# Moving the second sequence's transposes of a first feed-forward from TensorE to 32x32 squares and 16 DMAs

## The chip, the cores and the metric

The kernel runs on one core of one Trainium2 chip. The metric is the time of one execution on the device in microseconds (us). Three runs of the kernel before are at hand, and one more execution was taken with the hardware profiler; all readings of durations come from that one. Engines are called PE (TensorE; PEld is its weight load), ACT (ScalarE), DVE (VectorE), POOL (GpSimd) and SP (SyncE, which here only issues DMAs).

## The reference

Two transformer layers with a layer norm behind each of four steps, on 2 sequences of 512 rows with 512 columns. What bears on the change is the end of the first attention and the first feed-forward:

```python
x = _layernorm(x + _L0_attn_ref(x, ...))     # linear attention that reads a memory M with 8 heads
x = _layernorm(x + _L0_ffn_ref(x, w_gate, w_up, w_down))
x = _layernorm(x + _L1_attn_ref(x, ...))     # softmax attention, one head of 128
x = _layernorm(x + _L1_ffn_ref(x, ...))      # SwiGLU feed-forward, 1376 wide

def _L0_ffn_ref(x, w_gate, w_up, w_down):    # the weights are ternary: -s, 0 or s
    xf = x.astype(jnp.float32) / 128.0
    gate = jnp.einsum('bsh,ih->bsi', xf, w_gate)
    up = jnp.einsum('bsh,ih->bsi', xf, w_up)
    inter = jax.nn.silu(gate) * up
    inter_q = jnp.trunc(jnp.clip(inter * 128.0, -128.0, 127.0)).astype(jnp.int8)
    down = jnp.einsum('bsi,hi->bsh', inter_q.astype(jnp.float32), w_down)
    return jnp.trunc(jnp.clip(down * 128.0, -128.0, 127.0)).astype(jnp.int8)
```

## The kernel before

The rows of the two sequences lie in eight tiles of 128 rows by 512 columns, four for each sequence (`order` lists them, sequence 0 first). Matrix products contract over the partitions, so each step needs the rows transposed: 512 columns become four blocks of 128 partitions (`NK`), each with 512 rows side by side.

**Reading the attention's memory** (`read`, L392 to L428) goes tile by tile. PE makes eight products of a tile, one for each head, into eight PSUM banks. ACT takes the denominators from them (L405), DVE inverts these (L409), and the products are scaled and added to the row tile: three by ACT (L414) and summed by POOL (L418), five by DVE in place (L423). At the end POOL adds the sum of the three to the tile (L427). One tile later `norm_a0` (L495) normalizes the tile: statistics on DVE (L135, L137), root on POOL (L143, L144), an offset on DVE (L503), and the norm itself on ACT (L504). For the last tile it follows at once. In between, ACT and DVE also check and divide the ternary weights: `check_up` compares, and `divided` (L506) writes a chunk of gate and up weights divided by its scale, two activations for each of 11 chunks of 128 inner columns. Three chunks are asked for within this loop, the others in the feed-forward; the order on ACT and DVE is a planner's, which moves what is ready forward, so that some are done earlier.

**Splitting the rows** (`split`, L254) serves the first feed-forward. For each of the four blocks, PE makes four transposes into a PSUM bank (L264), ACT copies the bank rounded to the fast float format (`xh`, L265), and DVE writes what the rounding left (`xl`, L266). The first sequence's blocks are made inside the reading, the second's inside the feed-forward.

**The first feed-forward.** `up(b, c)` (L560) makes, for sequence b and chunk c, eight gate products (`pg_f`, L567: xh and xl of four blocks) and eight up products (`pu_f`), in one of two ways that a flag chooses. ACT then applies Silu (L583), DVE multiplies (L586) and cuts to 12 bits (L155), ACT makes two truncated halves (L165, L166) and DVE joins them (L593). The order of these calls is written out by hand at the end (L675 to L725): three chunks of the first sequence, the second sequence's split, a fourth chunk of the first, then three chunks of the second, and from there in turns. Each `up` also divides one further half chunk of weights (`to_divide`).

Beside it goes the preparation of the down weights. SP loads eleven chunks (`down_weights`, L248). DVE takes the largest value of the first chunk (`largest`, `mx_d`), PE and DVE make one scale of it (`over_partitions`, `scales`, which gives `inv_d`), POOL divides the eleven chunks by it (`check_down`, L435), DVE compares each (L204), and `verdict` makes the flag for `down`. The divided down weights lie in the places of up weights that are no longer needed. `f0_down` then makes the down products, the residual sum and the norm of each tile.

Pools matter for the change. `xtp` has two places of 8 KB a partition (tag "xt"), used by transposed rows. `wop` has six places of 4 KB (`pair_tile`), `wqp` four of the same size (`query_tile`). PSUM has eight banks, of which an `up` holds two.

A `with tc.issue_after(step.ins)` puts the instructions inside it behind `step` on its own engine's queue, without a wait. POOL's queue is in the order of the program.

Of the kernel before, what the change touches and what calls it, by code (L numbers as in the profile page):

```python
# [19 lines left out]
P = 128  # L20
# [9 lines left out]
LAST = HID - 1  # L30
LENT = 3
# [5 lines left out]
def kernel(  # L37
# [118 lines left out]

    def truncated_parts(pool, y, n, name):

        a = pool.tile([P, S], I8, tag="tr_a", name=f"ta_{name}")
        b = pool.tile([P, S], I16, tag="tr_b", name=f"tb_{name}")
        nc.scalar.activation(a[:n], y, AF.Relu, bias=below_half[:n])  # L165
        nc.scalar.activation(b[:n], y, AF.Relu, bias=below_half[:n], scale=-1.0)  # L166
        return a, b
# [86 lines left out]
    def split(b):  # L254

        hi = xtp.tile([P, NK, S], F32, tag="xt", name=f"xh_{b}").bitcast(F32R)
        los = [pair_tile(f"xl_{b}_{i}").bitcast(F32R) for i in range(2)]
        his = [hi[:, k, :] for k in range(NK)]
        los = [los[k // 2][:, k % 2, :] for k in range(NK)]

        def block(k):
            pt = psum(f"pt_f0{b}_{k}")
            for t in range(NT):
                nc.tensor.transpose(pt[:, ts(t, P)], xs[b][t][:, ts(k, P)], ident)  # L264
            nc.scalar.copy(his[k], pt)  # L265
            nc.vector.tensor_sub(los[k], pt, his[k].bitcast(F32))  # L266

        return his + los, block

# [11 lines left out]
    with tc.tile_pool(name="a0w", bufs=1) as a0w, tc.tile_pool(name="a0", bufs=2) as a0:  # L281
# [110 lines left out]
        def read(b, t, between):  # L392
# [34 lines left out]
            nc.gpsimd.tensor_add(x[:, :LAST], x[:, :LAST], ys[0][:, :LAST])  # L427
# [38 lines left out]
        for h in range(NH):  # L466
            queries(1, xt1, h)
            if h == 0:
                sum_weights(nc.vector, 4)
                sum_weights(nc.gpsimd, 5)  # L470
                fold(0)
                fold(1)
                mx_up = largest(
                    [gus[0][:, a].rearrange("p k i -> p (k i)") for a in range(2)], "up"
                )
# [71 lines left out]

    wdp = ctx.enter_context(tc.tile_pool(name="wdp", bufs=1))
    wds = down_weights(wd0_in, "0")
    with tc.tile_pool(name="f0", bufs=2) as f0:  # L550
# [9 lines left out]
        def up(b, c, behind=()):  # L560
# [19 lines left out]
            with ExitStack() as tied:  # L580
# [3 lines left out]
            y = f0.tile([P, S], F32, tag="y", name=f"y_f0{b}_{c}")  # L584

            step = nc.vector.scalar_tensor_tensor(  # L586
                y[:n], sg[:n], eff_up[:n, 1:2], pp[1][:n], ALU.mult, ALU.mult
            )
# [46 lines left out]
        pds, ys, stats, moved = {}, {}, {}, {}  # L635

        def scaled(i):
            y = f0.tile([P, HID], F32, tag="y", name=f"yd_{i}")
            moved[i] = nc.scalar.activation(y, pds[i], AF.Copy, scale=down_scale)
# [47 lines left out]
        top_d = over_partitions(mx_d, "down")  # L687
        for c in range(4, 8):
            up(0, c)
            if c == 4:  # L690
                sc_d, inv_d = scales(top_d, "down")
            up(1, c - 1)
            for i in range(2 * c - 8, 2 * c - 6):
                check_down(i)
        up(0, 8)
        up(1, 7)
        check_down(8)
        check_down(9)
        up(0, 9)
        check_down(10)  # L700
        up(0, 10)
        tot_d = total(counts_d, "down")
        up(1, 8)
# [3 lines left out]
        up(1, 9)  # L707
# [4 lines left out]
        up(1, 10, moved.values())  # L712
# [568 lines left out]
```

## Time and profile before

| what | value |
|---|---|
| median of 3 runs | 472.01 us (471.8, 472.01 and 799.53) |
| the profiled execution | 471.99 us, of which the span from first to last instruction is 470.0 us |
| PE busy / DVE busy / ACT busy / POOL busy | 463.0 / 327.9 / 268.1 / 114.4 us |
| granted TensorE clock | 0.996 |
| reading of the memory, first to last product | about 72 to 131 us |
| up part of the first feed-forward | about 131 to 219 us |
| down weights, SP's loads | 137.7 to 143.5 us |

The span is what the profile sees; some 2 us lie around it. A busy share is a mean over stages with different limits, so the stage around the change is read by itself, by its windows and by the chain of waits. A PE that is busy is not always at its own pace, since the ends of matrix products are modelled.

### The profile page before, as it was taken

What the parts mean: (1) busy time and instruction counts of PE and PEld (TensorE: products, weight loads), DVE (VectorE), ACT (ScalarE), POOL (GpSimd) and SP (SyncE); (2) the same over time, 40 slices, a digit from 0 to 9 for tenths busy, and PEclk for the clock granted to TensorE, in tenths of its full rate; (3) what the DMA queues carried; (4) which work ended last, traced back from release to release, by engine and by line L of the source; (5) the groups of instructions that cost most, each with busy time, mean ns of one, the idle gap of its engine ahead of it and who ended that gap; (6) DMA issues with size and microseconds to landing.
All of it is one profiled execution on the core that took longest, in us unless ns stands there. A gap on an engine that the chain in (4) does not pass through costs nothing.

```text
span 470.0 us, 5725 instructions
## 1 busy us (share of the span) xinstructions
PE 463.0 (99%) x1899; PEld 330.7 (70%) x1899; DVE 327.9 (70%) x622; ACT 268.1 (57%) x507; POOL 114.4 (24%) x141
## 2 busy tenths in 40 slices
PE   9999999999999999999999999999999999999995
PEld 8454444434478788888866568888888888888885
DVE  1265677767857677755988989986666767998633
ACT  3344799557556877645756743575644768532201
POOL 0343101566460090400348032000000000041101
PEclk9999999999999999999999999999999999999998
DMA  8999800000015000213192000000000000001011
GB/s 311 373 348 382 301 2 0 0 0 3 1 54 188 3 1 1 92 47 81 58 360 94 0 1 1 1 0 1 1 0 1 0 1 1 1 24 45 22 46 45
DMA packets 15187, 33.97 MB, mean 72 GB/s; under 512 B 3440, under 2 KB 4336, under 8 KB 15152
## 3 DMA queue, kind: packets, MB, share of 16 engines
q1 hardware_dynamic: 14864, 33.14, 19.6%
q8 instruction: 22, 0.36, 0.3%
q10 hardware_dynamic: 288, 0.36, 0.2%
q14 instruction: 13, 0.11, 0.1%
HBM read 31.40 MB, written 2.10 MB: 71 GB/s over the span
## 4 chain that ended last, share of the span: by engine, by line
PE 72%; ACT 7%; DVE 5%; issue 3%; POOL 0%; POOLq 0%; DVEq 0%; ACTq 0%
PE pm L1071 17%; PE pg_f L567 9%; PE pu_f L567 8%; PE pc L1071 8%; PE pdm L1159 7%; PE pd_f L622 4%; PE pdc L1159 4%; DVE x L423 4%; PE pqk L853 3%; PE po L401 2%; ACT y L414 2%; ACT t L433 2%; PE pv L866 2%; PE pot L949 1%; PE po L965 1%
## 5 line engine op out<-in xcount | busy, mean ns | idle before, releaser
L401 PE MATMUL po<-mw,q 128*128 128x512 f32 x128 | 57.1, 598 | 0.3 <-DVE mv_a L137 0.2
L325 PE MATMUL pq<-xt_a,wq 128*128 128x512 f32 (+1 forms) x152 | 56.9, 526 | 0.0
L143 POOL TENSOR_TENSOR rstd_f<-mv_f,ln_eps 128x1 f32<-128x1 f32 x15 | 4.4, 295 | 172.1 <-DVE mv_f L1174 130.2
L401 PEld LDWEIGHTS po<-mw,q 128*128 128x128 f32 x128 | 23.0, 189 | 32.1 <-issue 17.7
L325 PEld LDWEIGHTS pq<-xt_a,wq 128*128 128x128 f32 x152 | 26.2, 190 | 27.3 <-issue 26.2
L1071 PE MATMUL pm<-r,ugu 128*128 128x512 f32 x152 | 37.7, 389 | 0.0
L1071 PE MATMUL pm<-r,it_early 128*128 128x512 f32 x144 | 36.7, 392 | 0.0
L1071 PEld LDWEIGHTS pm<-r,ugu 128*128 128x128 f32 x152 | 28.5, 188 | 5.9
L1071 PEld LDWEIGHTS pm<-r,it_early 128*128 128x128 f32 x144 | 27.0, 188 | 6.0 <-issue 0.5
L423 DVE SCALAR_TENSOR_TENSOR x<-po,den,x 128x511 f32<-128x511 f32 x40 | 29.8, 745 | 1.9
L165 ACT ACTIVATE ta_f<-y_f,below_half 128x512 int8<-128x512 f32 (+1 forms) x22 | 15.9, 723 | 23.7 <-DVE y_f L155 23.3
L1081 DVE SCALAR_TENSOR_TENSOR ev_q<-pm,ev_q 128x512 f32<-128x512 f32 x27 | 18.6, 687 | 14.1 <-PE pm L1071 14.1
L418 POOL TENSOR_TENSOR y<-y,y 128x511 f32<-128x511 f32 x16 | 20.3, 1272 | 31.5 <-ACT y L414 30.8
L593 DVE SCALAR_TENSOR_TENSOR it_f<-tb_f,ta_f 128x512 fp32r<-128x512 int16 (+1 forms) x22 | 15.2, 690 | 16.3 <-ACT tb_f L166 16.3
L361 ACT ACTIVATE e<-pq,bq 128x512 f32<-128x512 f32 x16 | 11.1, 691 | 24.1 <-PE pq L325 21.7
L567 PE MATMUL pg_f<-xh,tu 128*128 128x512 f32 x88 | 24.7, 401 | 0.0
L1080 ACT ACTIVATE ev_q<-pc 128x512 f32<-128x512 f32 x27 | 16.0, 594 | 14.1 <-PE pc L1071 14.0
L435 POOL TENSOR_SCALAR td<-wd,inv_down 128x512 fp32r<-128x512 f32 x11 | 18.6, 1710 | 22.0 <-DVE inv_down L199 22.0
L567 PE MATMUL pg_f<-xl,tu 128*128 128x512 f32 x88 | 23.6, 390 | 0.0
L567 PE MATMUL pu_f<-xh,tu 128*128 128x512 f32 x88 | 23.6, 389 | 0.0
L567 PE MATMUL pu_f<-xl,tu 128*128 128x512 f32 x88 | 23.5, 389 | 0.0
L961 ACT ACTIVATE x<-x,off_f,rstd_f 128x512 f32<-128x512 f32 x7 | 5.7, 816 | 27.7 <-POOL off_f L960 27.7
(310 smaller groups left out, 1088.3 us busy)
## 6 DMA issues: line engine op xcount, KB each, us to landing
gu<-in_gu SPq DMA_DIRECT2D x20, 512.0 KB, 8.0
wo<-in_wo SPq DMA_DIRECT2D x16, 512.0 KB, 5.7
wd<-in_wd SPq DMA_DIRECT2D x20, 256.0 KB, 4.9
wq<-in_wq SPq DMA_DIRECT2D x8, 256.0 KB, 4.1
x<-in_x SPq DMA_DIRECT2D x7, 256.0 KB, 4.4
out<-x SPq DMA_DIRECT2D x7, 256.0 KB, 2.0
wqkv<-in_wqkv SPq DMA_DIRECT2D x1, 768.0 KB, 10.7
m<-in_m SPq DMA_DIRECT2D x1, 512.0 KB, 5.8
```

The source lines that it names most:

```text
L165: nc.scalar.activation(a[:n], y, AF.Relu, bias=below_half[:n])
L325: done = nc.tensor.matmul(pq[:, at], wq[h][:, k, :], xt[:, k, at], start=(k == 0), stop=(k == NK - 1),)
L401: nc.tensor.matmul(po, qs[b][h0 + j][:, ts(t, P)], mw[:, h0 + j, :], start=True, stop=True,)
L418: nc.gpsimd.tensor_add(ys[0][:, :LAST], ys[0][:, :LAST], y[:, :LAST])
L423: steps.append(nc.vector.scalar_tensor_tensor(x[:, :LAST], four[j][:, :LAST], d, x[:, :LAST], ALU.mult, ALU.add))
L435: eng.tensor_scalar(out, w, factor, None, ALU.mult)
L567: nc.tensor.matmul(pp[a], t[:, a, i % NK, :], x2[b][i], start=(i == 0), stop=(i == 2 * NK - 1),)
L622: nc.tensor.matmul(pd, inter[b][c][:, ts(t, P)], td[c].bitcast(F32R), start=(c == 0), stop=(c == last),)
L1071: nc.tensor.matmul(p, w, x, start=(left[id(p)] == begun[id(p)]), stop=(left[id(p)] == 1))
L1080: nc.scalar.activation(ev, pc, AF.Copy, scale=CROSS)
L1081: nc.vector.scalar_tensor_tensor(ev, pm, MAIN, ev, ALU.mult, ALU.add)
L1159: nc.tensor.matmul(p[:, :w], got[j // 4][1][kind][:, j % 4], down_parts[j][kind][:, cols], start=(j == 0 and kind == kinds[0]), stop=(j == ...
```

## The change

There are four parts.

- The second sequence's rows are no longer transposed by PE. DVE transposes each of its four tiles within squares of 32 by 32 (`turn_squares`), into one tile `squares`, each as soon as it is normalized. Then 16 DMAs (`move_squares`) put the squares where they belong in a tile `xt1`: nine issued by SP, three by ACT, four by POOL. Each moves 32 partitions with 16 runs of 128 bytes. `split(1, xt1)` reads `xt1` in place of PSUM. Four chunks of the first sequence now come before these reads, and two more, six in all (`LEAD`), before the second sequence's first chunk; the Silu and product of those two are queued behind the reads. The eleven loads of down weights are queued on SP behind its last move.
- `divided` is asked for six chunks in the attention's reading instead of three, and later chunks are divided whole, behind the second sequence's chunk that frees the place.
- For the last tile, the sum of L427 is on DVE.
- The maximum of the down weights is behind the second sequence's first chunk, the scale behind its third (`up(1, 2)`); the comparisons follow in the new loop.

```diff
+SQ = 32
+LEAD = 6
...
+    cut_off = {}
...
-        nc.scalar.activation(b[:n], y, AF.Relu, bias=below_half[:n], scale=-1.0)
+        cut_off[name] = nc.scalar.activation(
+            b[:n], y, AF.Relu, bias=below_half[:n], scale=-1.0
+        )
...
-    def split(b):
+    def split(b, xt=None):
...
         def block(k):
-            pt = psum(f"pt_f0{b}_{k}")
-            for t in range(NT):
-                nc.tensor.transpose(pt[:, ts(t, P)], xs[b][t][:, ts(k, P)], ident)
-            nc.scalar.copy(his[k], pt)
-            nc.vector.tensor_sub(los[k], pt, his[k].bitcast(F32))
+            h, l = his[k], los[k]
+            if xt is None:
+                rows = psum(f"pt_f0{b}_{k}")
+                for t in range(NT):
+                    nc.tensor.transpose(rows[:, ts(t, P)], xs[b][t][:, ts(k, P)], ident)
+            else:
+                rows = xt[:, :, k, :]
+                h, l = (u.rearrange("p (t q) -> p t q", t=NT) for u in (h, l))
+            return (
+                nc.scalar.copy(h, rows),
+                nc.vector.tensor_sub(l, rows, h.bitcast(F32)),
+            )
...
+    def move_squares(squares, xt):
...
+        src = squares.rearrange("p t (k i) -> p (t k) i", k=NK)
+        dst = xt.rearrange("p t k i -> p (t k) i")
+        for i in range(P // SQ):
+            for j in range(P // SQ):
+                eng = nc.gpsimd if i == j else nc.scalar if i == (j + 2) % 4 > 0 else nc.sync
+                dma = eng.dma_start(dst[ts(j, SQ), :, ts(i, SQ)], src[ts(i, SQ), :, ts(j, SQ)])
+                if eng is nc.sync:
+                    last = dma
+        return last
...
-            nc.gpsimd.tensor_add(x[:, :LAST], x[:, :LAST], ys[0][:, :LAST])
+            if (b, t) == order[-1]:
+                steps.append(nc.vector.tensor_add(x[:, :LAST], x[:, :LAST], ys[0][:, :LAST]))
+            else:
+                nc.gpsimd.tensor_add(x[:, :LAST], x[:, :LAST], ys[0][:, :LAST])
...
-                t = query_tile(f"tu_{c}").bitcast(F32R)
+                t = (pair_tile if c in PAIRED else query_tile)(f"tu_{c}").bitcast(F32R)
...
+        PAIRED = (LEAD - 2, LEAD - 1, len(CHUNKS) - 1)
...
+        def turn_squares(i):
+            b, t = order[i]
+            nc.vector.transpose(squares[:, t, :], xs[b][t])
...
-            if i in (3, 4, 5):
+            if i >= len(order) - LEAD:
                 for a in range(2):
-                    divided(i - 3, a)
+                    divided(i - len(order) + LEAD, a)
             if i == 5:
                 parts, block = split(0)
                 x2.append(parts)
+                squares = xtp.tile([P, NT, HID], F32, tag="xt", name="squares")
...
+            if i > NT:
+                turn_squares(i - 1)
         norm_a0(len(order) - 1, steps)
+        turn_squares(len(order) - 1)
...
+    xt1 = fp.tile([P, NT, NK, P], F32, tag="it11", name="xt_f01", bufs=1)
+    moved = move_squares(squares, xt1)
     wdp = ctx.enter_context(tc.tile_pool(name="wdp", bufs=1))
-    wds = down_weights(wd0_in, "0")
+    with tc.issue_after(moved.ins):
+        wds = down_weights(wd0_in, "0")
...
-            if to_divide:
-                part = to_divide.pop(0)
-                if part:
-                    divided(*part)
+            for part in to_divide.get((b, c), ()):
+                divided(*part)
...
-        to_divide = [(c, a) for c in range(3, len(CHUNKS)) for a in range(2)]
+        to_divide = {
+            (1, c - LEAD): [(c, a) for a in range(2)] for c in range(LEAD, len(CHUNKS))
+        }
...
-        to_divide[2:2] = [None, None]
-        for c in range(3):
-            up(0, c)
-        parts, block = split(1)
+        for c in range(LEAD - 2):
+            up(0, c, [cut_off[f"f00_{c - 2}"]] if c > 1 else ())
+        parts, block = split(1, xt1)
         x2.append(parts)
-        for k in range(NK):
-            block(k)
-        step = up(0, 3)
+        moved = [ins for k in range(NK) for ins in block(k)]
+        for c in range(LEAD - 2, LEAD):
+            up(0, c, moved)
+        step = up(1, 0)
         with tc.issue_after(step.ins):
             mx_d = largest([wds[0]], "down")
-        for c in range(3):
+        up(1, 1)
+        last = len(CHUNKS) - 1
+        for c in range(LEAD, last + 1):
+            up(0, c)
+            if c == LEAD:
+                top_d = over_partitions(mx_d, "down")
+            up(1, c - LEAD + 2)
+            if c == LEAD:
+                sc_d, inv_d = scales(top_d, "down")
+            for i in range(2 * (c - LEAD), 2 * (c - LEAD) + 2):
+                check_down(i)
+        check_down(last)
+        for c in range(last - LEAD + 3, last - 1):
             up(1, c)
-        top_d = over_partitions(mx_d, "down")
...
         tot_d = total(counts_d, "down")
-        up(1, 8)
         flag_d, eff_d = verdict(tot_d, sc_d, "down")
...
-        up(1, 9)
+        up(1, last - 1)
         ternary_d = branch(flag_d)
```

Two smaller edits: in `up`, the product of L586 is queued behind the same steps as the Silu, and for chunks 2 and 3 of the first sequence both stand behind the truncation (L166) of the chunk two before. The maximum of the first layer's up weights is queued behind the last copy of the transposed rows of the second sequence in the attention.

More of the change, by code (lines that the diff above doesn't have):

```diff
@@ L472 @@
                 fold(1)
-                mx_up = largest(
-                    [gus[0][:, a].rearrange("p k i -> p (k i)") for a in range(2)], "up"
-                )
+                with tc.issue_after(copies[-1].ins):
+                    mx_up = largest(
+                        [gus[0][:, a].rearrange("p k i -> p (k i)") for a in range(2)], "up"
+                    )
             elif h == 1:
@@ L583, in up @@
                 nc.scalar.activation(sg[:n], pp[0][:n], AF.Silu, scale=silu_scale[:n])
[L584 to L588, printed above, removed]
+                y = f0.tile([P, S], F32, tag="y", name=f"y_f0{b}_{c}")
+                step = nc.vector.scalar_tensor_tensor(
+                    y[:n], sg[:n], eff_up[:n, 1:2], pp[1][:n], ALU.mult, ALU.mult
+                )
             cut_to_12(y[:n])
@@ L632, in down @@
             return pd
-        pds, ys, stats, moved = {}, {}, {}, {}
+        pds, ys, stats, scaling = {}, {}, {}, {}
         def scaled(i):
             y = f0.tile([P, HID], F32, tag="y", name=f"yd_{i}")
-            moved[i] = nc.scalar.activation(y, pds[i], AF.Copy, scale=down_scale)
+            scaling[i] = nc.scalar.activation(y, pds[i], AF.Copy, scale=down_scale)
             cut_to_12(y)
@@ L673, in normed @@
                 layernorm_apply(xs[b][t], xs[b][t], stats[i])
-        to_divide[2:2] = [None, None]
-        for c in range(3):
-            up(0, c)
-        parts, block = split(1)
+        for c in range(LEAD - 2):
+            up(0, c, [cut_off[f"f00_{c - 2}"]] if c > 1 else ())
+        parts, block = split(1, xt1)
         x2.append(parts)
-        for k in range(NK):
-            block(k)
-        step = up(0, 3)
+        moved = [ins for k in range(NK) for ins in block(k)]
+        for c in range(LEAD - 2, LEAD):
+            up(0, c, moved)
+        step = up(1, 0)
         with tc.issue_after(step.ins):
             mx_d = largest([wds[0]], "down")
-        for c in range(3):
-            up(1, c)
-        top_d = over_partitions(mx_d, "down")
[L688 to L701, printed above, removed]
+        up(1, 1)
[11 more added lines that the diff above has]
+        for c in range(last - LEAD + 3, last - 1):
+            up(1, c)
         tot_d = total(counts_d, "down")
-        up(1, 8)
         flag_d, eff_d = verdict(tot_d, sc_d, "down")
@@ L710 @@
             f0_down(i)
-        up(1, 10, moved.values())
+        up(1, last, scaling.values())
         for i in range(2, len(order) - 2):
```

## The prediction

> **What bounds the kernel now.** I read the page first, for what is busy; then the chain of waits in order of time around the feed-forward, for what the removed work costs there; then the timeline of each engine around the last tile of the attention, for when the second sequence's rows are ready; then the windows and the DMA view, for slack and for the price of small packets.
>
> ```profile
> span 470.0 us, 5725 instructions
> PE 463.0 (99%) x1899; PEld 330.7 (70%) x1899; DVE 327.9 (70%) x622; ACT 268.1 (57%) x507; POOL 114.4 (24%) x141
> ```
>
> TensorE has work on it for 99% of the span. Only two things can move the end: work taken from its stream, or a wait put into it.
>
> The chain of waits, in order of time (start, length, what), where the second sequence's rows are turned:
>
> ```profile
> 140.33 1.82 PE pu_f L567 x8
> 142.15 1.42 PE pt_f L264 x13
> 143.57 1.85 PE pg_f L567 x8
> 145.43 1.82 PE pu_f L567 x8
> 147.25 0.33 PE pt_f L264 x3
> 147.58 2.10 PE pg_f L567 x8
> 149.68 1.82 PE pu_f L567 x8
> ```
>
> The chain is TensorE alone: the 16 transposes stand in it with 1.42 + 0.33 us. Undisturbed, eight gate products take 1.81 us; the chunk behind the transposes took 2.10.
>
> The timeline around the last tile (start, length, engine, line, what; in brackets the idle time before):
>
> ```profile
> 134.68 1.60 DVE L423 SCALAR_TENSOR_TENSOR x<-po,den,x 128x511 f32<-128x511 f32 x2
> 136.37 1.30 POOL L427 TENSOR_TENSOR x<-x,y 128x511 f32<-128x511 f32 x1 [0.80 <-DVE x L423]
> 137.70 0.70 DVE L135 BATCH_NORM_STATS2 st_a<-x 128x6 f32<-128x512 f32 x1 [1.29 <-POOL x L427]
> 139.80 0.82 ACT L504 ACTIVATE x<-x,off,rstd_a 128x512 f32<-128x512 f32 x1 [0.53 <-DVE off L503]
> ```
>
> The last tile is complete at 140.62. TensorE started the feed-forward at 131.21 with the first sequence, so this lateness costs nothing today. It matters to whatever must be done between it and the second sequence's first product.
>
> Busy time by stage (window, length, then busy us of each engine, clock, DMA share, GB/s): the attention's reading and the first feed-forward.
>
> ```profile
> 72.00:131.20 59.20, 58.85 (x149) 25.30 (x148) 42.47 (x96) 39.80 (x108) 31.07 (x33) 1.00 0.00 1
> 131.20:215.00 83.80, 83.80 (x379) 68.83 (x378) 56.70 (x112) 55.35 (x90) 26.00 (x23) 1.00 0.19 61
> ```
>
> VectorE and ScalarE have 27 and 28 us free in the second window. The DMA engines are nearly empty.
>
> The nearest thing to the new moves is a load of short rows near 219 us. Issue lengths in ns, queue totals of a burst of it, and sizes with time to landing:
>
> ```profile
> L740 SPq DMA_DIRECT2D gu<-in_gu x1: 508/508/508, 219.6 to 219.6; - x1
> ...
> q1 hardware_dynamic: 616, 0.12, 116.6%
> ...
> gu<-in_gu SPq DMA_DIRECT2D x1, 128.0 KB, 3.6
> gu<-in_gu SPq DMA_DIRECT2D x1, 64.0 KB, 3.9
> ```
>
> The second line covers 221.1 to 221.6: 616 packets in 0.5 us, or 1,230 a us over 16 engines. Taken over all three short-row loads, 1,584 packets went from about 220.2 to 223.4, only some 495 a us. These are my two ends for packet speed.
>
> **What the Trainium skill says.** "DMA: Bandwidth & Descriptors", section "Why small descriptors are slow (HBM only)", says that transfers from SBUF to SBUF escape the penalty of small packets, and gives 78% of a link for 1 MB in 128-byte packets. No row here moves SBUF to SBUF; the load from memory is my nearest. The same page, "Issuing engines are not separate DMA queues", says that queues of several engines share the 16 DMA engines and save issue time alone. "SBUF — State Buffer", under "SBUF: two separate sides", says that for a DMA issued by GpSimd software writes the descriptors, and that VectorE in a two-port mode locks it out meanwhile. No DMA is issued by GpSimd in this trace. "VectorE: DVE Perf Modes", "The three transpose paths", says that VectorE transposes only within 32x32 squares, which is why the squares must be moved.
>
> **The change part by part.** Profiled execution: 471.99 us, 1.99 around a span of 470.0; the median of the runs is 472.01, the same.
>
> *Transposes gone.* 16 on TensorE: 1.42 + 0.33 = 1.75 us. The slow chunk behind them: 2.10 - 1.81 = 0.29. Sum: -2.04 us. Both are on the path.
>
> *Rows ready.* The last sum moves from POOL (1.30 us) to VectorE, by the two-input rows of 0.68 us. VectorE's last product ends at 136.28 and `off` at 136.4, so the sum ends near 137.0, statistics 137.7, aggregate 137.9, POOL's root 138.8, `off` 139.05. ScalarE's first Silu ends at 139.26; the norm then takes 0.82, to 140.1: 0.5 us earlier than 140.62. The four squares' transposes are not in this trace. Below, 0.43 us (the cut at L155, same size); above, 0.69 (a two-input row); I take 0.68. The first two lie in gaps of 2.1 us in which VectorE waits for `den`, the third beside the statistics; the fourth ends near 140.8. Say 141.0 with semaphores.
>
> *The moves.* 16 DMAs, each 32 partitions x 16 runs = 512 packets of 128 bytes: 8,192 packets. SP issues nine: 9 x 0.54 = 4.9 us, until 145.9; ScalarE three at about 0.5, where it has slack; POOL four. Start to first packet was about 1.0 us in the short-row load, last packet to landing about 0.4. At 1,230 packets a us: 6.7 us, all landed at T = 141.0 + 1.0 + 6.7 + 0.4 = 149.1. At 495: 16.5 us, T = 158.9. The first rate held only with a full queue and short runs; the second contains the thinning end of a load from memory, which 12 queued moves don't have until their end. I take 8 us, T = 150.5.
>
> *What waits for T.* Four ScalarE copies and four VectorE differences, in steps of 0.6 us: the last difference ends at T + 0.7 + 3 x 0.6 + 0.7 = T + 3.2. TensorE now runs six chunks of the first sequence before the second: 131.2 + 6 x 3.63 = 153.0. It wants the last difference for its eighth product, at 153.0 + 7 x 0.227 = 154.6. So its wait is T - 151.3 where positive. At 150.5 it is nothing. Queued behind the eight are Silu and product of chunks 4 and 5. Those hold four PSUM banks and the second sequence's first two chunks the other four, so TensorE meets that backlog only at chunk 6, from 160.3.
>
> *Early weights.* Two more chunks of `divided` (four activations in steps of 0.61 us) move ahead of the feed-forward; of tu_3's two, the trace shows them before 84 us already. ScalarE has 59.2 - 39.8 = 19.4 us free in the reading, and VectorE 16.7 for its transposes. But TensorE is not at its pace there: 128 halves at 0.43, plus 1.9 for transposes and the flag, are 56.9 of 58.9 us; 2 us go to late PSUM releases. In-order insertions can add to that: between nothing and 1.5; I take 0.3.
>
> *Down weights and down scale.* SP issues the eleven loads behind its nine moves, from about 146 instead of 137.7, and they land within about 10 us. Their first user, the maximum, is now behind the second sequence's first chunk, near 157. The scale follows TensorE's tenth chunk instead of an earlier one: inv_down near 168.3, 5 us later. POOL then has 11 x 1.7 = 18.7 us of divisions, and a memset between them that waits for chunk 14 (182): 182 + 7 x 1.7 = 194. The sum is wanted near 203.8, so nothing is on the path; 9.8 us of cover.
>
> Sum: 472.0 - 2.04 + 0.3 + 0 = **470.3 us**.
>
> **Rivals.** *The packets are slow* (T near 158.9). For it: a mean of 495 a us is what this trace has over a whole load. Against: the burst is 2.5 times faster, and the source is SBUF. Wait 7.6: 472.0 - 2.0 + 0.3 + 7.6 = 477.9.
>
> *POOL's queue sets T.* One mechanism on the other side: software must write four times 512 descriptors, one move after another, at a price p that no row shows; the load issues of SP and ScalarE cost 0.33 to 0.51. T = 141 + 4p + 1.4. The gain is gone at T = 153.0, p = 2.7 us; 2% is lost at T = 162.4, p = 5.0. At p = 5.5: T = 164.4, wait 13.1, 472.0 - 2.0 + 0.3 + 13.1 = 483.4. For it: VectorE's cut runs beside it and may lock it out. Against: POOL has nothing else until 163, and p at 1 to 2 us would end it before SP's moves.
>
> *The gain is eaten in the reading*: the insertions delay `den` and so PSUM releases by 1.5 us. 472.0 - 2.0 + 1.5 = 471.5. For it, ScalarE runs without a gap from 75 to 83; against, the idle time behind that.
>
> **How the numbers follow.** In time: 0.50; slow packets 0.27; POOL 0.14; eaten 0.09. The likeliest is 470.3, its own range 469.5 to 472. To hold 8 in 10, I take in the slow packets with their worse half and leave POOL's upper part out: 469.2 to 480. About 2% (9.4 us) is what a measurement of this kernel can tell from no change. No case gains that, since the path loses 2 us at most; 0.01 for what I have not seen. Slower by that much is POOL's case and a thin end of the packets': 0.15.
>
> **What would show it.** Right: no L264 of the second sequence; 16 moves landed by about 151; the copies and differences done before 154; no pause over 0.5 us before the second sequence's first gate products; chunk 6 starting near 160. Wrong: a TensorE gap at 153 with ScalarE's copies waiting for a DMA; POOL's issues at several us each; or po bubbles before 131, with the feed-forward starting later than 131.5.

## The result, and the profile after

| kernel | median | ratio to before, 95% interval | profiled span | first gate product to first down product | end of last output's issue to end of span |
|---|---|---|---|---|---|
| before | 472.04 us (8 runs) | 1 | 470.0 us | 79.69 us | 2.57 us |
| after | 470.69 us (8 runs) | 0.9966 [0.9956, 0.9976] | 468.7 us | 77.58 us | 3.39 us |
| after, once more, on the chip of a later experiment | 470.71 us (7 runs) | 0.9967 [0.9955, 0.9979] | 468.7 us | 77.56 us | 3.39 us |

The change takes 1.3 us off by the medians, 0.3%. The forecast was 470.3 us. The last two columns are read from the trace, the fourth between start times and the fifth from the end of that issue: the stage that was changed gained 2.1 us, and the closing part of the program gave 0.8 us back. The one time of 799.53 us among the runs of before lies far off the others and takes no part in the ratio.

The page's first lines of the kernel after:

```profile
span 468.7 us, 5727 instructions
PE 461.0 (98%) x1883; PEld 329.0 (70%) x1883; DVE 329.5 (70%) x627; ACT 267.5 (57%) x507; POOL 115.1 (25%) x144
```

PE has 16 instructions fewer and is busy 2.0 us less. DVE has five more (four squares, one sum) and POOL three more in number.

The chain of waits after, in order of time (start, length, what), from the fifth chunk's second half on:

```profile
149.40 1.81 PE pg_f L611 x8
151.21 1.81 PE pu_f L611 x8
153.02 1.81 PE pg_f L611 x8
154.84 1.81 PE pu_f L611 x8
156.65 1.81 PE pg_f L611 x8
...
208.40 4.99 PE pd_f L666 x22
```

The second sequence's first gate products start at 153.02, where six undisturbed chunks of 3.63 us from 131.22 put them (153.0). No `pt_f` stands between the chunks, and every group of eight takes 1.81 us. In the kernel before, the first down products stood 2.10 us later in the same view:

```profile
210.50 4.99 PE pd_f L622 x22
```

How the squares moved, in the kernel after, by the instructions that name the tile `squares` (count, then min/median/max length in ns, first and last start in us):

```profile
L292 SPq DMA_DIRECT2D xt_f<-squares x9: 627/645/1769, 141.3 to 148.2; - x9
L551 DVE STREAM_TRANSPOSE squares<-x x4: 694/711/712, 122.1 to 140.4; 128x512 f32<-128x512 f32 x4
L292 POOL DMA_DIRECT2D xt_f<-squares x4: 648/654/996, 141.9 to 144.2; - x4
L292 ACTq DMA_DIRECT2D xt_f<-squares x3: 643/655/731, 141.2 to 142.6; - x3
...
DMA to landing us min/median/max: 2.1/3.5/4.4
```

SP is the last: its ninth issue starts at 148.2, and that move lands at 150.25. ACT and POOL had issued their shares by 143.3 and 144.8. What waited for the moves, by the timeline of ACT and DVE:

```profile
141.19 2.10 ACTq L292 DMA_DIRECT2D xt_f<-squares  x3
143.34 0.72 ACT L169 ACTIVATE ta_f<-y_f,below_half 128x512 int8<-128x512 f32 x1 [2.36 <-DVE y_f L157]
...
150.23 0.71 ACT L170 ACTIVATE tb_f<-y_f,below_half 128x512 int16<-128x512 f32 x1
150.84 2.17 ACT L278 CAST xh<-xt_f 128x512 fp32r<-128x512 f32 x4
151.58 2.50 DVE L279 TENSOR_TENSOR xl<-xt_f,xh 128x512 fp32r<-128x512 f32 x4
```

The last two lines carry no bracket of idle time: ACT came from the truncation at 150.23 and went straight on. So the copies did not wait for the moves, which had landed 0.6 us before; they stood in ACT's own queue behind the truncations, and the first of these stood behind ACT's three issues, which end at 143.29. (The bracket of 2.36 us names DVE, but that value was ready at 141.5, and in the kernel before the same truncation started at 141.35.) The last difference ends at 154.08, and the eighth gate product wants it at 154.6. The cover is 0.5 us.

Busy time by stage after, in the same two windows as before (length, busy us of PE, PEld, DVE, ACT, POOL, clock, DMA share, GB/s):

```profile
72.00:131.20 59.20, 58.87 (x149) 25.28 (x148) 43.79 (x98) 42.09 (x112) 31.05 (x33) 1.00 0.00 1
131.20:215.00 83.80, 83.80 (x372) 69.01 (x371) 58.00 (x116) 53.99 (x89) 27.03 (x26) 1.00 0.26 73
```

The reading holds 2.3 us more of ACT (the weights divided early) and 1.3 us more of DVE (squares), and is not longer: PE starts the feed-forward at 131.22, and at 131.21 before.

### The profile page after: what moved, and what is told of

Read it like the earlier page. It is cut to its first block, busy times and chain, and to the rows that moved or that the text cites. A ratio compares the mean times of both kernels' runs of the same rounds, so it can differ in the third digit from the quotient of the medians.

```text
span 468.7 us, 5727 instructions
## 1 busy us (share of the span) xinstructions
PE 461.0 (98%) x1883; PEld 329.0 (70%) x1883; DVE 329.5 (70%) x627; ACT 267.5 (57%) x507; POOL 115.1 (25%) x144
## 4 chain that ended last, share of the span: by engine, by line
PE 71%; ACT 7%; DVE 5%; issue 3%; POOL 0%; POOLq 0%; DVEq 0%; ACTq 0%
PE pm L1111 17%; PE pg_f L611 9%; PE pu_f L611 9%; PE pc L1111 8%; PE pdm L1199 7%; PE pd_f L666 4%; PE pdc L1199 4%; DVE x L450 3%; PE pqk L893 3%; PE po L428 2%; ACT y L441 2%; ACT t L463 2%; PE pv L906 2%; PE pot L989 1%; PE po L1005 1%
```

## The experiments

**1. The transposes back on TensorE, everything else as after.** `squares` and its moves are left out; `split(1)` transposes on PE again, behind the same four chunks.

```diff
-                squares = xtp.tile([P, NT, HID], F32, tag="xt", name="squares")
...
-    moved = move_squares(squares, xt1)
-    with tc.issue_after(moved.ins):
-        wds = down_weights(wd0_in, "0")
+    wds = down_weights(wd0_in, "0")
...
-        parts, block = split(1, xt1)
+        parts, block = split(1)
```

> The changed kernel with the second sequence's 16 transposes back on TensorE (into PSUM, in the new order of chunks), and without squares, moves and xt1; the down weights are loaded as early as before. Theory (the gain is the 16 transposes and the pause behind them, about 2.05 us of TensorE, and about 0.75 us of it is lost at the end of the program because POOL issues DMAs): TensorE's last product ends about 2 us later than in the changed kernel, the end of the program is 0.75 us shorter, time about 472.0. Rival (the gain comes from the new order of chunks and the weights divided earlier): the time stays at 470.7 or falls to 470.0.

Measured: 471.63 us, ratio 0.9990 [0.9984, 0.9997], span 469.6; first gate to first down product 79.40 us. The chain of waits of this kernel:

```profile
145.64 1.42 PE pt_f L273 x13
147.07 1.85 PE pg_f L604 x8
148.92 1.82 PE pu_f L604 x8
150.74 0.33 PE pt_f L273 x3
151.07 1.85 PE pg_f L604 x8
```

The transposes have the lengths of before, 1.42 and 0.33 us, but the group behind the second part takes 1.85 us, and not 2.10. So the 2.11 us of the stage split into 0.29 us that the new order alone brings (79.69 to 79.40) and 1.82 us that the moves bring (79.40 to 77.58): the 1.75 us of transposes and 0.07 us more. Less the 0.82 us that the closing part takes (it is 2.57 us here, as before), the moves gain 1.0 us of time; the two ratios, 0.9990 and 0.9966, give 1.1. The rival, that the gain comes from the new order and the early weights, falls but for the 0.29 us.

**2. No DMA on POOL.** The four squares on the diagonal stay in their partitions, so POOL can copy them:

```diff
+                if i == j:
+                    nc.gpsimd.tensor_copy(dst[ts(i, SQ), :, ts(i, SQ)], src[ts(i, SQ), :, ts(i, SQ)])
+                    continue
...
```

> The changed kernel with the four moves of diagonal squares, which POOL issued as DMAs and which stay on their own partitions, made as four copies on POOL. POOL then issues no DMA. Theory (a queue of POOL lengthens the end of the program by about 0.75 us): TensorE as in the changed kernel, from the last output's issue to the end of the span 2.7 us in place of 3.5, time about 470.0. Rival (the 0.75 us were chance in one profile): 470.7. If four copies of 32x512 took over 2 us each, the second sequence would wait and the time rise above 471.

Measured: 470.29 us, ratio 0.9954 [0.9941, 0.9967], span 468.7, closing part 3.16 us. The timeline of POOL:

```profile
141.51 2.70 POOL L292 COPY xt_f<-squares 32x512 f32<-32x512 f32 x4 [1.98 <-DVE squares L554]
```

Four copies take 2.70 us, the four DMA issues took 2.94. Without any DMA of POOL the stage is as long as after (77.59 us), so POOL's queue costs nothing in it. The closing part falls by 0.23 us only, to 3.16, where 2.7 was expected, so that queue is not the main cause of the 0.8 us.

**3. The kernel before with one small POOL DMA** (128 x 1), to look at the same question from the other side.

```diff
+    nc.gpsimd.dma_start(fill[:, 8:9], ln_eps)
```

> The kernel before with one DMA more, 128x1 numbers from one constant tile to an unused column of another, issued by POOL ahead of the feed-forward, where nothing waits for it. Theory (any DMA of POOL costs at the end of the program): TensorE as before, the end 0.5 to 0.8 us longer, time about 472.7. Rival (chance, or the number of moves matters and not the queue): 472.0.

Measured: 472.11 us, ratio 1.0002 [0.9992, 1.0011], closing part 2.62 us against 2.57. So a DMA from POOL does not by itself lengthen the end by the 0.5 to 0.8 us that were expected.

**4. All sixteen moves on SP.** This tells apart what sets the landing: the runs of 128 bytes, which are the same, or the issues, which are now in one row.

```diff
-                eng = nc.gpsimd if i == j else nc.scalar if i == (j + 2) % 4 > 0 else nc.sync
+                eng = nc.sync
```

> The changed kernel with all 16 moves issued by SP. Theory (the rate of issues sets the landing, 0.68 us a move): 16 issues take some 11 to 12 us from 141.3, the last lands near 154.8, TensorE waits about 3.5 us before the second sequence's first chunk, the end of the program is 0.75 us shorter: about 473.4. Rival (packets of 128 bytes on the DMA engines set the landing): the landing stays near 150.5 and the time is 470.0.

Measured: 474.61 us, ratio 1.0037 [1.0020, 1.0054], span 473.0; first gate to first down product 82.45 us, 4.87 more than after. SP issued from 141.63 to 153.13 and the last move landed at 154.6. ACT and PE waited, by the timelines of this kernel:

```profile
154.74 2.18 ACT L278 CAST xh<-xt_f 128x512 fp32r<-128x512 f32 x4 [3.80 <-DMA xt_f<-squares]
155.41 2.33 PE L611 MATMUL pg_f<-xh,tu 128*128 128x512 f32 x4 [2.07 <-ACT xh L278]
```

The same 8,192 runs landed 4 us later because seven more issues stood in SP's row. There were even more small packets (POOL's four moves had gone in larger ones, see the last section), and still each of the last twelve moves landed 2.1 us after its issue had started, so that no packets queued up. So issues set the landing, not packets. The wait does not explain the whole 4.87 us. Its windows (busy columns as above, the clock third from the right):

```profile
156.00:157.00 1.00, 0.95 (x3) 0.33 (x3) 1.00 (x3) 1.00 (x3) 0.00 (x0) 1.00 1.02 311
157.00:158.00 1.00, 1.00 (x3) 0.81 (x4) 1.00 (x3) 1.00 (x2) 0.00 (x0) 0.52 0.97 334
158.00:159.00 1.00, 1.00 (x4) 0.81 (x3) 1.00 (x2) 0.08 (x1) 0.00 (x0) 0.50 1.03 320
160.00:161.00 1.00, 1.00 (x5) 0.75 (x5) 0.05 (x1) 1.00 (x3) 0.00 (x0) 0.78 1.05 379
```

After the wait TensorE's clock was granted at half for some 3.4 us. Half of that, 1.7 us, is lost time. The wait formula gives 3.0 us (this kernel's feed-forward starts at 131.54, 0.3 us later than after, so 154.6 - 151.6). Together 4.7 us, beside 4.87 measured.

The seven runs themselves show the two parts. Five took 474.25 to 475.05 us with a mean clock of 0.994 or 0.995, the profiled one among them; two took 472.47 and 472.66 us with 0.998 and 0.997, while 3.41 us at half would leave 0.996 at most. So the same wait did not always bring the clock down, and where it did, the run was about 2 us longer. Without it the time is hardly above that of the kernel before (median 471.96 on this chip).

**5. One chunk less ahead of the second sequence.** Five chunks of the first sequence instead of six take 3.63 us from the cover.

```diff
-LEAD = 6
+LEAD = 5
...
-            for i in range(2 * (c - LEAD), 2 * (c - LEAD) + 2):
+            for i in range(2 * (c - LEAD), min(2 * (c - LEAD) + 2, last)):
```

> The changed kernel with LEAD = 5: five chunks of the first sequence, not six, before the second sequence's first, and five chunks of weights divided early. Theory: the landing stays where it was, near 150.4, and TensorE wants the second sequence 3.6 us earlier, at 149.4. The last difference is needed at 151.0 and ready at 153.7 to 154.1, so TensorE loses 2.7 to 3.1 us, and more if its clock falls after the wait as in the run with all moves on SP (0.50 for 3.4 us, some 1.7 us): 473.4 without that, 475.1 with it. Rival (the sixth chunk has nothing to do with the cover, the landing isn't what is waited for): 470.7.

Measured: 475.58 us, ratio 1.0077 [1.0053, 1.0100], span 473.6; the stage takes 83.25 us, 5.67 more than after. What TensorE waited for, in the stage:

```profile
PE pg_f L611 <- ACT xh L278: 1.8, 1, 1.8
PE pg_f L611 <- ACT tu L463: 1.3, 1, 1.3
```

The first wait is the one that the sixth chunk covers. The second, at 190 us, is a weight chunk that ACT divides late, since one chunk fewer was divided in the reading. The clock, by the windows:

```profile
151.00:152.00 1.00, 0.98 (x3) 0.56 (x2) 1.00 (x3) 1.00 (x3) 0.00 (x0) 0.58 0.98 379
153.00:154.00 1.00, 1.00 (x3) 0.75 (x3) 1.00 (x3) 0.27 (x1) 0.00 (x0) 0.50 1.05 383
...
191.70:193.00 1.30, 1.30 (x7) 1.04 (x7) 1.21 (x4) 1.16 (x3) 0.56 (x1) 1.00 0.02 6
```

It fell behind the wait of 1.8 us and did not behind that of 1.3. The second sequence's first chunk ended at 156.37, 3.9 us later than six chunks from the start at 130.66 would. The formula gives 2.8 us of it (T = 149.93, one chunk less, a start 0.56 us earlier: T - 147.1); the remaining 1.1 us is put down to the clock, whose slow stretch lay in part beside the wait for copies. That split is less sure than in experiment 4: one of the four runs took 475.53 us with a mean clock of 0.999, and it was not profiled. So the sixth chunk is what makes the moves free; the number of chunks ahead was no detail.

**6. The last tile's sum back on POOL.**

```diff
-            if (b, t) == order[-1]:
-                steps.append(nc.vector.tensor_add(x[:, :LAST], x[:, :LAST], ys[0][:, :LAST]))
-            else:
-                nc.gpsimd.tensor_add(x[:, :LAST], x[:, :LAST], ys[0][:, :LAST])
+            nc.gpsimd.tensor_add(x[:, :LAST], x[:, :LAST], ys[0][:, :LAST])
```

> The changed kernel with the last tile's sum back on POOL. Theory: the last tile is normalized 0.2 to 0.6 us later and the moves land so much later; the last difference ended 0.5 us ahead of its product in the changed kernel, so TensorE waits for 0 to 0.3 us and the time is 470.7 to 471.0. Rival (the sum on DVE was part of the gain): 471.4 or more.

Measured: 471.69 us, ratio 0.9985 [0.9976, 0.9994], span 470.1; the stage takes 78.75 us, 1.17 more than after. Timelines of ACT, DVE and PE:

```profile
152.62 2.16 ACT L278 CAST xh<-xt_f 128x512 fp32r<-128x512 f32 x4
153.36 2.50 DVE L279 TENSOR_TENSOR xl<-xt_f,xh 128x512 fp32r<-128x512 f32 x4
153.29 2.06 PE L608 MATMUL pg_f<-xh,tu 128*128 128x512 f32 x4
```

POOL's sum takes 1.30 us where DVE's takes 0.69, and the last square ends 0.65 us later, counted from the start of the feed-forward. ACT's copies start 1.36 us later. They did not wait for the moves, the last of which had landed at 151.42, but stood straight behind ACT's truncations, and those behind ACT's three issues:

```profile
142.26 2.81 ACTq L292 DMA_DIRECT2D xt_f<-squares  x3
145.11 0.72 ACT L169 ACTIVATE ta_f<-y_f,below_half 128x512 int8<-128x512 f32 x1 [3.05 <-issue]
```

The three took 2.81 us, one of them 1.35, where they took 2.10 after. So 0.65 us of the 1.36 are the later square, and 0.71 us the longer issue, whose cause stays open. PE's first four products then follow ACT's copies at 0.5 us each and take 2.06 us instead of about 0.9. There is no single pause, and the clock stays at 1.00. The expectation of at most 0.3 us was wrong: it counted the moves' landing alone and not ACT's queue. The cover after is 0.5 us, so this small edit of the change carries about 1.0 us of its gain (0.9 by the two ratios).

**7 and 8. What the end consists of.** The trace's semaphore instructions show two things behind the last output's issue that differ from before. SP's last six waits come in a row behind the landing, at 0.06 us each, where before three of them were met earlier: 0.3 us. And POOL stands still for 0.34 to 0.37 us ahead of one of its closing instructions. That pause is ahead of POOL's 197th recorded instruction after, in experiment 2 and in experiment 6, which have 199, 197 and 200, though it is a different instruction in each; kernels with 196 or fewer have none. Experiment 7 is experiment 2 with two memsets moved to DVE (196 recorded on POOL, 194 in experiment 8); experiment 8 is experiment 7 with four of the input loads cut in two, which moves SP's round of semaphores on by four.

```diff
-    nc.gpsimd.memset(fill[0:1, 0:1], 0.0)
+    nc.vector.memset(fill[0:1, 0:1], 0.0)
...
-        nc.gpsimd.memset(counts_d, 0.0)
+        nc.vector.memset(counts_d, 0.0)
```

> As the run with four copies on POOL, with two memsets (an unused tile's first number, and the counts) moved from POOL to DVE, so that POOL has 195 recorded instructions in place of 197. Theory: in the changed kernel and in that run POOL stood still for 0.33 to 0.4 us ahead of its 197th instruction, in the closing steps, which the kernels with fewer don't have[...]; without that the end falls from 3.16 to about 2.8 us, time about 469.9. Rival (the pause goes with ACT's or POOL's part in the moves): end 3.16 us, time 470.3.

> As the run with fewer POOL instructions, and four loads of the attention's constants (wqkv, bqk, wo1, bo) cut into two each, which adds four DMAs of SP where SP has nothing else. Theory: SP's closing waits go through the completion semaphores in a fixed order, and the twelve new DMAs shifted them so that the last output's is waited for first and six others follow it at 0.06 us each; four more DMAs, 16 in all, a multiple of the eight semaphores, restore the order of before. The end falls to 2.55 us, time about 469.6. Rival (it's not the order): the end stays at 2.8 us.

Measured: closing parts of 2.85 and 2.58 us (3.16 in experiment 2, 2.57 before). POOL's pause is gone in the first, SP's row of waits too in the second, as expected. The 0.82 us thus split into 0.23 us that leave with POOL's DMAs (experiment 2), 0.31 with the pause and 0.27 with the row of waits. Experiments 1 and 4 agree: with no moves, or with sixteen on SP and none on POOL, the closing part is 2.57 and 2.56 us. But the times, for which 469.9 and 469.6 were expected, are 470.19 us, ratio 0.9958 [0.9941, 0.9975], and 470.37 us, ratio 0.9961 [0.9946, 0.9976]: not told apart from experiment 2 at 0.9954 or from after at 0.9966. In the profiled executions, the time that lies around the span is 2.45 and 2.21 us in these two, and 1.82 us in experiment 2. What leaves the closing part seems to come back outside the span, at least in part. Experiment 7's shorter span (467.5 us) is for the most part a feed-forward that started 0.9 us earlier than in experiment 2; that start lies between 130.0 and 131.2 us in the profiles of before, after and experiments 1 to 9.

**9. The pause put into the kernel before.** Six more memsets of 128 x 1 give POOL 199 instructions.

```diff
+        for u in range(6):
+            nc.gpsimd.memset(fill[:, 8 + u : 9 + u], 0.0)
```

> The kernel before with six small memsets (128x1) added to POOL's stream in the middle of the first feed-forward, so that POOL has 199 instructions instead of 193; nothing waits for them. If a fixed place in POOL's stream (its 197th instruction) costs 0.3 to 0.4 us at the end of the kernel, the closing part grows from 2.57 to about 2.9 to 3.0 us, the pause stands ahead of POOL's 197th instruction, and the time is 472.0 + 0.35, about 472.3 to 472.4. If the pause comes from the change itself (its DMAs, its squares), the closing part stays at 2.6 us and the time at 472.0.

Measured: closing part 3.02 us; a pause of 0.35 us stands ahead of the 197th instruction. The place in the stream is thus shown, in a kernel that has none of the change. The time is 472.37 us beside 472.27, ratio 1.0005 [0.9991, 1.0018]: too small to be seen in it.

**10. The first sequence's rows in squares too.** If the moves bring 1.8 us for one sequence, the other's transposes lie in the reading, 2 x 0.88 us. On top of experiment 8: four more squares, sixteen moves by SP, copies from the moved tile. The query tiles are allotted in fours, so that one of their places holds the moved rows.

```diff
+            if 0 < i <= NT:
+                turn_squares(i - 1)
+            if i == NT:
+                xt0 = a0.tile([P, NT, NK, P], F32, tag="q", name="xt_f00", bufs=4)
+                move_squares(squares[0], xt0, True)
+            if i == 6:
+                parts, block = split(0, xt0)
...
+                for k in range(NK):
+                    block(k)
```

> The kernel with POOL's copies, fewer POOL instructions and four more loads, and besides the FIRST sequence's rows turned in squares too: four more square transposes on VectorE in the reading, 16 moves all issued by SP (nothing else is on SP there), the four rounded copies and differences from the moved tile at the end of the seventh tile's reading. Tile 3 is normalized at about 107.9 us; its square at 108.7; 16 issues of 0.65 us and one long one to 120.3; last landing near 122.5; copies and differences in the gaps of ScalarE and VectorE until about 127; the first gate product wants them at 129. Main theory: the reading is TensorE's own pace, so its 16 transposes (2 x 0.88 us) come off the path: 470.4 - 1.75 = 468.6 us. Rival 1: late PSUM releases take the place of the transposes, 470.4 us. Rival 2: copies, differences and the later squares of the second sequence crowd the end of the reading; TensorE waits at the start of the feed-forward or of the second sequence, and its clock falls after the wait: 472 us or more.

Measured: 480.49 us, ratio 1.0178 [1.0160, 1.0196]: rival 2. From the first product's start to the last one's end the reading shrank from 58.9 to 56.3 us; then PE waited:

```profile
138.19 2.36 PE L628 MATMUL pg_f<-xh,tu 128*128 128x512 f32 x4 [9.69 <-ACT xh L278]
```

SP issued from 114.69 to 126.36, one tile later than I had worked out, because the fourth tile is normalized only at 113.9; and the copies stood behind the last norm in ACT's queue. The clock was at half from 131.6 to 141.8.

**11.** The changed kernel on this chip is the third row of the table above.

> The changed kernel itself, on the same chip as the version with both sequences in squares, so that the two can be compared through the same runs of the kernel before: 470.7 us and a ratio of 0.9966 again.

**12. The same with the moves in three parts and the copies ahead of the last denominators.**

```diff
-                move_squares(squares[0], xt0, True)
+                    move_squares(squares[0], xt0, slice(0, 2))
+                    move_squares(squares[0], xt0, slice(2, 3))
...
+                    move_squares(squares[0], xt0, slice(3, 4))
...
+                        if halves and h0:
+                            tied.enter_context(tc.issue_after(halves[3][0].ins))
```

> The kernel with both sequences in squares, with the two things mended that its trace showed late: the first sequence's squares are moved in three parts (tiles 0 and 1, tile 2, tile 3; 16 moves each, all on SP), so that little is left to move when tile 3 is normalized near 113.9 us; and the copies and differences of the first sequence are queued ahead of the last four denominators of the reading instead of behind the last norm. In the first attempt the last product of the reading ended near 128.5 us, 56.3 us after its first (58.3 in the changed kernel), and TensorE then waited 9.7 us for the copies. Expected now: last landing near 122, copies 126 to 128.2, differences until 129.4 where the eighth product wants the last at about 130.2, so no wait: 2.0 us less than the 470.4 of the version with POOL's copies and four more loads, 468.4 us. Rival: the 48 issues of SP are no shorter than the 0.63 us of the whole moves, tile 3's squares land near 127 or later, TensorE waits some 3 us with its clock falling behind that: 472 to 474 us.

Measured: 478.33 us, ratio 1.0112 [1.0094, 1.0130]: the rival, and worse than it said. SP's, ACT's and PE's timelines:

```profile
100.52 32.21 SPq L297 DMA_DIRECT2D xt_f<-squares  x48
134.13 2.18 ACT L278 CAST xh<-xt_f 128x512 fp32r<-128x512 f32 x4 [5.25 <-DMA xt_f<-squares]
134.80 2.36 PE L642 MATMUL pg_f<-xh,tu 128*128 128x512 f32 x4 [6.75 <-ACT xh L278]
```

Issues of 128 and 256 runs take 0.60 us (median), issues of 512 runs 0.63 in experiment 10. Cutting the moves in three made 48 issues of nearly the same length, and 32 us of issuing. The reading again ended after 56.4 us, 2.5 less than after, so up to 2.5 us are there for the first sequence; neither version reached them. It is an upper bound: in both versions the first sequence's copies and differences came only after the reading, while after has them inside it. (The 58.3 us for the changed kernel in the expectation is a slip; it is 58.9.) A version that shares out these issues, or copies the diagonal on POOL, was not tried, and whether the gain can be had stays open. None of the twelve runs is shown to beat the changed kernel.

## Why the prediction was right

The size holds: 470.3 us forecast, 470.69 measured. The main mechanism holds too: 1.82 us of the gain are the transposes that left TensorE's path. That the total came so near is in part luck, as two errors in the moves and two in the sum cancel. Step by step:

- *Transposes gone, 1.75 us*: right. Experiment 1 gives 1.82 us for the moves.
- *The slow chunk behind them, 0.29 us*: right in size, wrong in its cause. Experiment 1 keeps the transposes and loses the pause. It came from the order before, not from the transposes.
- *Reading, +0.3 us*: the measured cost is 0.0 us. The insertions found gaps, as the windows show.
- *Rows ready at 141.0*: 141.16. A square took 0.71 us; 0.68 was taken.
- *The moves, T = 150.5*: the copies found everything landed at 150.84, and the last one landed at 150.25, so T is right, but by two errors that cancel. An issue took 0.645 us and one of the nine 1.77, 7.5 us in all, not 4.9; and it is SP's row of issues that sets T (experiment 4), not packets at 1,024 a us. There were 6,144 packets of 128 bytes, not 8,192, as POOL's moves went in larger ones; they took 11 to 13 ns each on their engine and ran beside the issues. From the last issue's start to landing it is 2.1 us. The 78% of a link that the prediction quotes is of a remote DMA, and no run here measures it.
- *Wait, T - 151.3*: right for the place and near for the slack (0.5 us left, 0.8 forecast; the terms as they stand give T - 151.4). But the copies did not start at T. The prediction gave ACT's three issues no cost, "where it has slack"; they held up ACT's queue, and the copies started 0.6 us behind the landing. Experiment 6 shows what this can cost. As a price of a real wait it was too low: experiments 4 and 5 lost 1.9 and 1.1 us beyond it in their profiles, with the clock at half. The rivals with waits of 7.6 and 13.1 us left such a loss out.
- *Down weights*: the scale at 168.3 and the end of POOL's divisions near 194 came as forecast (168.4 and 194.7). The cover of 9.8 us did not: DVE's own order put the last comparison at 201.5 and had the total at 203.0, and the weight load of PE's test product came at 204.1 without waiting. Some 1.1 us of cover were left.
- *Not in the sum*: the closing part, +0.82 us in the profile. The stage gained 2.1 us where 1.74 was forecast; the end took that difference and 0.4 us more, by which the total lies above the forecast.
- *What a measurement can tell, 2%*: too coarse. The interval of the ratio, 0.9956 to 0.9976, tells 0.3% from no change.

Of the rivals, slow packets are ruled out by experiment 4, which moved the same runs over SP's queue alone, in more small packets, where they landed as fast as SP issued them. POOL's queue had p = 0.65 us for each issue but the first (1.0), far from the 2.7 at which the gain would be gone; a lock-out by VectorE, which was busy beside it, did not show, and experiment 2 has the same stage without it. The gain eaten in the reading is ruled out by the start of the feed-forward at 131.22. What nearly decided instead was a case that I had not priced: with one chunk less ahead (experiment 5) the change is slower than before, and with all issues on SP (experiment 4) too, where the clock falls.

## What to carry to other kernels

Work that TensorE does for layout can go to VectorE and DMAs, but the gain is the work's own length and not more, and it is kept only if the detour is covered to the last half microsecond; count the chunks that cover it against the longest row of issues at about 0.7 us from one to the next, some 1 us for the longer issue that each row here had, and 1.4 us from the end of the last issue to its landing. Share such issues among queues, and do not cut them finer: an issue costs nearly the same for 128 runs as for 512. But an issue also holds up its own engine's queue: what stands behind it there, here ACT's truncations and copies, is late by its length. Giving ACT fewer of the moves was not tried alone. On a kernel bound by TensorE, price a wait of about 2 us with another 1 to 2 us for a clock that may fall behind it.

## What the runs showed of the hardware

- The clock can fall behind a single wait of 1.8 us (experiment 5) or 2.1 us (experiment 4, in five runs of seven). It did not behind one of 1.3 us, nor behind four short ones with a total of 1.2 us (experiment 6). It then stayed at 0.50 for 3.41 us.
- The length of the wait alone does not decide. In the clock records of the traces that were read for this (before, after and experiments 4, 5, 6, 10 and 12) every stretch between two changes is a whole multiple of 3.413 us: 3.41 us at half in experiments 4 and 5, 10.24 in 10 and 12, and 460.80 at full after. In the 3.41 us that end with the fall, TensorE had products for 22% of the time (experiment 4) and 35% (experiment 5), counting 0.227 us for each. In the stretches of the same grid that hold the two waits without a fall it had 54% (experiment 5, 188.7 to 192.1) and 74% (experiment 6, 153.8 to 157.2). So where a wait lies on this grid should matter, which would explain the two shorter runs of experiment 4; that is inferred and not shown, since they were not profiled. The Trainium skill, "TensorE: Matmul & The Clock Gate", section "Part 1: The HAM clock gate", gives half the clock after an idle window of some 3.4 us and the full clock after as much sustained work, with windows that run freely. The grid and the return agree. That the whole window must be idle does not fit 22% and 35% of work, and the measurement decides.
- SP's issue of a move from SBUF to SBUF took 0.60 to 0.65 us for 128, 256 and 512 runs of 128 bytes alike. "DMA: Bandwidth & Descriptors", section "Issuing engines are not separate DMA queues", says that several queues save issue time alone; experiment 4 agrees, with 4 us of it. It adds that this time is not always small beside the transfer: here it set the landing.
- A DMA issued by POOL moves the same runs in other packets. Its queue (packets, MB, share of 16 engines) and its moves, by the DMA view of after:

```profile
q0 software_dynamic: 128, 0.26, 0.3%
...
xt_f<-squares SPq DMA_DIRECT2D x9, 64.0 KB, 2.4
xt_f<-squares POOLq DMA_DIRECT2D x4, 64.0 KB, 3.8
xt_f<-squares ACTq DMA_DIRECT2D x3, 64.0 KB, 3.9
```

  In the trace, 64 of these packets hold 4,096 bytes each and took 159 ns at the least and 294 ns in the median, where the other queues moved 6,144 packets of 128 bytes. An issue cost POOL 0.65 us (1.0 us for the first), no more than SP.
- POOL stands still for 0.34 to 0.37 us ahead of its 197th recorded instruction, whatever that is (after, and experiments 2, 5, 6, 9, 11 and 12; the other kernels have 196 or fewer and no such pause). What it does in that time stays open: in after, neither of the two queues that the trace calls `instruction` moves anything between 449 and 469.0 us, and the pause ends at 468.3.
